# Values of two token tiles at once by a Strassen product in a gated window-attention kernel

## The chip, the cores and the metric

The kernel runs on one core of a Trainium2 chip. The metric is the device time of one execution in microseconds, the median of the runs shown. The core has five engines with an instruction queue each, worked off in order: TensorE (PE, with its weight loads listed as PEld), VectorE (DVE), ScalarE (ACT), GpSimd (POOL) and SyncE (SP, which here only issues DMAs).

## What is computed

The input x has 8 sequences of 1024 tokens with 512 channels, all in float32. With xn the layer norm of x (no scale, no shift), the reference is:

```python
q, k, v = (xn @ W.T + bias for each of Wq, Wk, Wv), cut into 16 heads of 32 channels
scores  = q k^T / sqrt(32), and -1e30 where (i mod 256) < (j mod 256)
s       = (softmax(scores) v, heads joined) @ Wo.T + bo
y       = clip((xn @ sign(weights).T) * scale + bias, -100, 100)
out     = x + s * silu(y)
```

## The kernel before

**Tiles.** A sequence (a batch b) is 8 tiles of 128 tokens. The tokens are permuted so that the mask, which depends on positions modulo 256, becomes a block triangle of tiles. `norm_work` normalises a tile and turns it, so that xnT holds channels on partitions. The products of a batch are: queries and keys (`heads_work`, for each of 4 groups of 4 heads and each half of the tokens), values (`values_work`, for each token tile), the gate y (`gate_work`, for each tile) and the output (`output_work`, for each tile). Apart from the gate each is written by `product` (L339): four chunks of 128 channels, and in each chunk four matmuls of 32 stationary columns side by side, 512 columns wide. They accumulate in one PSUM bank. A product may be cut inside a chunk into two column ranges.

**Steps.** The main loop (L1053) has 8 batches x 4 head groups g x 9 steps n. A step does, in this order on PE:

- `probs_quad`: the *t* matmuls, scores with the row maximum already subtracted, into a tile of four PSUM banks. ACT then takes the exponential of it (L612).
- `attend_quad`: probabilities times values (*av*) of the step before, at some steps `sum_keys`, and filler. This is the first stretch of filler, "gap one".
- at steps 0 and 7 `shift_rows` turns the parts of the row maxima (*mT*, L555), and ACT copies them (L557).
- `maxima_quad`: the *s* matmuls, scores of the next head group, into the same four-bank tile. DVE takes their row maximum (`pm`, L528).
- filler again, "gap two", up to the next step's t matmuls.

POOL adds up the exponentials of a group over the keys (`add_probs`, L643). Step n's additions are issued in step n + 1; there are none for step 0. The probabilities have two buffers beside the two tiles of sums, so an exponential can wait for the additions of two steps before.

**Filler.** Everything else is filler: queries, keys, values, gates, outputs, turns. Its order is written out by hand, one string for each head group (L787 to L804): `V4` is the value product of tile 4, `G2` the gate of tile 2, `q20` the queries of group 2 and half 0, `O4` the output of tile 4 of the batch before, `N0` the norm of a half, `W0` a turn of the output weights, `R` the product that folds the value bias into the output bias; a prime means the next batch, and what stands before a bar may be begun in the group before. `Beside.fill` (L919) takes filler from this list until a wanted cost is reached. An item has a cost in microseconds (0.86 for a chunk, 2.0 for a gate), may be unready, may be split, and may be free (cost 0: loads, splits, finishing operations).

**PSUM.** Eight banks: four for the t and s tile, two for av, and two ("bank", L121) that all filler products and mT share in turn. A bank comes free when its product has been read: values by one ACT copy (L377), queries and keys by one ACT operation with bias (L394), gates by two DVE operations (L426, L427), outputs by two DVE operations (L722, L723), whose result POOL adds to x (L724) before SP stores it, mT and the key sums by an ACT copy.

**Gates.** A gate's xn is split by ACT (L421) and POOL (L422) into two parts, which have two buffers each, and multiplied by the sign weights in two passes.

**Weights.** The turned weights of queries, keys, values, gate and output lie in SBUF all the time.

## Time and profile before

| | us |
|---|---|
| three runs | 2245.12, 2246.44, 2246.84 |
| median | 2246.44 |
| the profiled execution | 2248.59 |
| its span, first to last instruction | 2246.7 |

| engine | busy us | share of the span |
|---|---|---|
| PE | 2196.6 | 98% |
| DVE | 1276.6 | 57% |
| ACT | 876.5 | 39% |
| POOL | 1323.7 | 59% |

Busy time is the time in which an engine executes. PE at 98% is busy, but matmuls side by side overlap, so the sums of single groups are larger than the time they take together. A line of the timeline has the start, the time until the last one ends, engine, line of the code, what is written and read, the form and the count; in brackets is the engine's idle time before it and what ended it. A line of the table by stretches has the stretch, its length, and for PE, PEld, DVE, ACT and POOL the busy time with the count of instructions; then the granted TensorE clock, the DMA share and GB/s. DMA moves 93.55 MB in the span, 42 GB/s.

### The profile page before, as it was taken

Reading aid. Unit: us, or ns where it says so; the run is one execution under the profiler, and the core shown is the slowest. Engines: PE = TensorE matmul, PEld = TensorE weight load, DVE = VectorE, ACT = ScalarE, POOL = GpSimd, SP = SyncE. Lnnn points to the kernel's source line nnn. Section 1 sums busy time; section 2 is a strip of 40 time slices with the busy share of each in tenths; the row PEclk is TensorE's granted clock in tenths of the full one; section 3 lists DMA queues with packets and bytes.
Section 4 is the critical chain, followed back from the end, with each engine's and each line's share of the span. In section 5 each row is a group of like instructions: output and inputs, shape, how many; then the busy total and the mean of one; then the engine's idle time right before and its main releaser. Section 6 shows DMA issues by size and latency. Waiting matters only on the chain. (4 is left out here: it accounts for less than half of the span.)

```text
span 2246.7 us, 56396 instructions
## 1 busy us (share of the span) xinstructions
PE 2196.6 (98%) x25553; PEld 851.8 (38%) x25553; DVE 1276.6 (57%) x1633; ACT 876.5 (39%) x864; POOL 1323.7 (59%) x1198
## 2 busy tenths in 40 slices
PE   8999999999999999999999999999999999999998
PEld 3334333343333433333333333334333343333333
DVE  4556556665556655566555665565655665555664
ACT  2235433434334434344333443334334344333331
POOL 1256566666566666576556665557666566655562
PEclk9999999999999999999999999999999999999999
DMA  4001000120001210012000120002100111000113
GB/s 164 1 16 34 11 6 29 53 76 30 25 25 39 72 33 25 25 62 68 16 25 25 62 67 16 25 26 66 62 16 27 41 62 62 7 20 25 44 53 123
DMA packets 49672, 93.55 MB, mean 42 GB/s; under 512 B 5388, under 2 KB 5656, under 8 KB 49432
## 3 DMA queue, kind: packets, MB, share of 16 engines
q1 hardware_dynamic: 48720, 88.76, 12.0%
q8 instruction: 200, 3.28, 0.6%
q10 hardware_dynamic: 712, 1.19, 0.2%
q14 instruction: 40, 0.33, 0.0%
HBM read 56.37 MB, written 33.55 MB: 40 GB/s over the span
## 5 line engine op out<-in xcount | busy, mean ns | idle before, releaser
L643 POOL TENSOR_TENSOR p<-p,p 128x512 f32<-128x512 f32 x930 | 1096.4, 1212 | 202.7 <-PE av L625 111.2
L528 DVE TENSOR_REDUCE pm<-s 128x4 f32<-128x2048 f32 (+3 forms) x384 | 664.9, 1752 | 608.8 <-PE s L515 605.9
L612 ACT ACTIVATE p<-t 128x2048 f32<-128x2048 f32 x288 | 540.9, 1878 | 856.4 <-PE t L599 797.8
L700 DVE RECIPROCAL aT<-aT 128x128 f32<-128x128 f32 x256 | 230.2, 928 | 222.4 <-ACT aT L661 222.4
L515 PE MATMUL s<-k,q 32*128 32x512 f32 (+3 forms) x3072 | 320.2, 510 | 7.8 <-ACT p L612 6.9
L625 PE MATMUL av<-p,v 128*32 128x512 f32 (+3 forms) x3072 | 308.2, 496 | 1.6 <-DVE aT L704 1.4
L599 PE MATMUL t<-q,k 32*128 32x512 f32 (+3 forms) x3072 | 306.1, 492 | 0.0
L351 PE MATMUL q_ps<-xnT,wqT 128*32 128x512 f32 (+2 forms) x2656 | 254.2, 497 | 5.5 <-ACT xnT L322 4.7
L351 PE MATMUL k_ps<-xnT,wkT 128*32 128x512 f32 (+2 forms) x2784 | 257.2, 487 | 1.1 <-ACT xnT L322 0.7
L351 PE MATMUL v_ps<-wvT,xnT 128*32 128x512 f32 (+3 forms) x2712 | 254.9, 491 | 0.0
L351 PE MATMUL o_ps<-woT,aT 128*32 128x512 f32 (+2 forms) x2584 | 244.6, 501 | 1.7 <-ACT xnT L322 0.7
L724 POOL TENSOR_TENSOR s<-s,xb 128x512 f32<-128x512 f32 x63 | 85.8, 1362 | 245.3 <-DVE s L723 245.3
L428 POOL TENSOR_SCALAR y<-y 128x512 f32<-128x512 f32 x64 | 39.6, 619 | 279.9 <-DVE y L427 265.2
L422 POOL TENSOR_TENSOR x<-xnT,x 128x512 fp32r<-128x512 f32 x58 | 74.0, 1277 | 166.4 <-ACT x L421 164.0
L599 PEld LDWEIGHTS t<-q,k 32*128 32x128 f32 x3072 | 139.1, 185 | 25.8
L351 PEld LDWEIGHTS k_ps<-xnT,wkT 128*32 128x32 f32 x2784 | 82.7, 110 | 170.4 <-issue 142.5
L351 PEld LDWEIGHTS q_ps<-xnT,wqT 128*32 128x32 f32 x2656 | 78.3, 109 | 177.3 <-issue 152.5
L625 PEld LDWEIGHTS av<-p,v 128*32 128x32 f32 x3072 | 70.3, 108 | 195.9 <-issue 163.4
L351 PEld LDWEIGHTS v_ps<-wvT,xnT 128*32 128x32 f32 x2712 | 78.6, 109 | 167.8 <-issue 143.9
L515 PEld LDWEIGHTS s<-k,q 32*128 32x128 f32 x3072 | 116.3, 185 | 59.4 <-ACT p L612 47.5
L449 PE MATMUL y_ps<-fwT,x 128*128 128x512 f32 x464 | 135.5, 418 | 1.7 <-ACT k L394 1.3
L351 PEld LDWEIGHTS o_ps<-woT,aT 128*32 128x32 f32 x2584 | 76.2, 109 | 156.7 <-issue 135.2
(95 smaller groups left out, 1465.2 us busy)
## 6 DMA issues: line engine op xcount, KB each, us to landing
x<-in_L_attn_x_dram SPq DMA_DIRECT2D x64, 256.0 KB, 3.2
g<-t SPq DMA_DIRECT2D x64, 256.0 KB, 2.0
gb<-g SPq DMA_DIRECT2D x64, 256.0 KB, 3.1
xb<-in_L_attn_x_dram SPq DMA_DIRECT2D x64, 256.0 KB, 3.1
out_dram<-s SPq DMA_DIRECT2D x63, 256.0 KB, 2.5
wk_st<-in_L_attn_Wk_dram ACTq DMA_DIRECT2D x2, 512.0 KB, 5.5
wq_st<-in_L_attn_Wq_dram SPq DMA_DIRECT2D x2, 512.0 KB, 4.6
wv_st<-in_L_attn_Wv_dram SPq DMA_DIRECT2D x2, 512.0 KB, 6.4
```

The lines of the kernel that those rows point to most:

```text
L351: nc.tensor.matmul(hold[0][cols, lo:hi], lhsT=lhsT[:, cols], rhs=rhs[:, lo:hi], start=(i == 0 and lo == 0), stop=(i == n - 1), skip_group_ ...
L422: nc.gpsimd.tensor_tensor(part[1], src, part[0].bitcast(F32), ALU.subtract)
L428: nc.gpsimd.tensor_scalar(y[0], y[0], MAX_VAL, -MAX_VAL, ALU.min, ALU.max)
L449: nc.tensor.matmul(hold[0], lhsT=part[i][:, c, :], rhs=wT["fw"][:, c, :], start=(i == 0 and c == 0), stop=(i == 1 and c == NC - 1),)
L515: nc.tensor.matmul(sc[:, h, at : at + w], lhsT=qt[b, g][head_rows(h), i * P : (i + 1) * P], rhs=kt[b, g][head_rows(h), lo:hi], start=not f ...
L528: nc.vector.tensor_reduce(pm[:, 0 if lo == 0 else 1, i, :], sc[:, :, at : at + w], AX.X, ALU.max)
L599: nc.tensor.matmul(sc[:, h, at : at + w], lhsT=kt[b, g][head_rows(h), j * P : (j + 1) * P], rhs=qt[b, g][head_rows(h), q0 : q0 + w], start ...
L612: nc.scalar.activation(pt[:, :, :width], sc[:, :, :width], AF.Exp, scale=SCALE)
L625: nc.tensor.matmul(av[b, g, f][head_rows(h), lo : lo + w], lhsT=vt[b, j][:, g * P + h * DK : g * P + (h + 1) * DK], rhs=pts[b, g, n][:, h, ...
L643: nc.gpsimd.tensor_tensor(t[:, hs, lo : lo + w], t[:, hs, lo : lo + w], p[:, hs, at : at + w], ALU.add)
L700: nc.vector.reciprocal(r, r)
L724: nc.gpsimd.tensor_tensor(s, s, xr, ALU.add)
```

## The change

**Values.** `values_work` is replaced by `values_pair`: the values of two token tiles i and j come from one Strassen product (in Winograd's form) on 2 x 2 blocks. The left blocks X are halves of the channels (2 x 128) of the two tiles, the right blocks A are quarters of the value weights (256 channels by 256 outputs). Seven block products take the place of eight. Each is 2 chunks of 128 channels, 256 columns wide, and so 14 half-wide chunks in place of the 2 x 4 full ones. They go in four phases through four banks, two block products to a bank, the last alone.

**Sums.** POOL makes four differences T of the left blocks for each pair (`prepare`, issued during the pair before). Four sums S of the weight blocks are made once, by DVE, at the start. The block products are combined by seven more sums of 256 columns for each pair: three read only SBUF and run on POOL, four read PSUM and run on DVE; ACT makes four copies of 256 columns in place of two of 512. DVE's first sum reads what POOL has added from the first phase.

**Weights.** Seven weight blocks (128 x 3584 float32) take more room than the value weights did, and now share one tile with the output weights (128 x 2048). Both are kept in DRAM after the start. `Lo` and `Lv` in the strings load one over the other, twice in each batch, on SP.

**Room.** The gate's two parts have one buffer each in place of two, so a gate is split only when the gate before it has been multiplied. The head outputs of the later half have five buffers in place of six.

**Order.** The strings are new: pairs replace single tiles, O4 to O7 stand at the start of group 1 and O0 to O3 at the start of group 2, and the output weights are turned earlier, in group 1 of batch 0. `Beside.fill` may stop ahead of an opening product after a slow bank, and at the end of gap one a slow half-chunk that is next and ready is finished there.

```diff
-    heads = pool("heads", 6)
+    heads = pool("heads", 5)
...
+    part_sums = pool("part_sums", 1)
+    sums_p = pool("sums", 1)
+    wvo = pool("wvo", 1)
...
+    kept_w = pool("kept_w", 1, space=bass.MemoryType.DRAM)
...
+    def sum_blocks():
+        for out, a, b, op in (
+            ("S1", "A21", "A22", ALU.add),
+            ("S3", "A11", "A21", ALU.subtract),
+            ("S2", "S1", "A11", ALU.subtract),
+            ("S4", "A12", "S2", ALU.subtract),
+        ):
+            nc.vector.tensor_tensor(wb[out], wb[a], wb[b], op)
...
+    def keep_weight(name):
+        weight_d[name] = kept_w.tile(list(wb["tile"].shape), F32, tag=name, name=f"{name}_d")
+        nc.sync.dma_start(weight_d[name], wb["tile"])
+        wb["name"] = name
+
+    def load_weight(name):
+        shared_tile(name)
+        nc.sync.dma_start(wb["tile"], weight_d[name])
+        wb["name"] = name
...
-    def values_work(b, it):
...
+            phases = (
+                (("X11", "A11"), ("T2", "S2")),
+                (("T3", "S3"), ("T1", "S1")),
+                (("T4", "A22"), ("X22", "S4")),
+                (("X21", "A12"),),
+            )
...
+                for q in range(NH):
+                    cols = head_rows(q)
+                    nc.tensor.matmul(
+                        hold[k][cols, part * 256 : part * 256 + 256],
+                        lhsT=self.t[lhs][:, c, cols], rhs=wb[rhs][:, c, :],
+                        start=(part == 0 and c == 0), stop=(c == 1), skip_group_check=True,
+                    )
...
+            for out, a, b in (
+                ("T1", "X12", "X11"), ("T2", "X22", "T1"), ("T3", "X22", "X12"), ("T4", "X21", "T2"),
+            ):
+                nc.gpsimd.tensor_tensor(t[out], t[a], t[b], ALU.subtract)
...
+            if k == 0:
+                u[0], u[1] = part_sum(name, 0), part_sum(name, 1)
+                nc.scalar.copy(u[0], ps[:, LO])
+                nc.scalar.copy(u[1], ps[:, HI])
+                later(lambda: plus(u[1], u[1], u[0], nc.gpsimd))
+            elif k == 1:
...
+                plus(u[2], ps[:, LO], u[1])
+                plus(vt[b, j][:, HI], ps[:, HI], u[2])
+                plus(u[3], ps[:, HI], u[1])
+            elif k == 2:
+                y21, y12 = vt[b, i][:, HI], vt[b, j][:, LO]
+                nc.scalar.copy(y21, ps[:, LO])
+                nc.scalar.copy(y12, ps[:, HI])
+                later(lambda: plus(y21, y21, u[2], nc.gpsimd))
+                later(lambda: plus(y12, y12, u[3], nc.gpsimd))
+            else:
+                plus(vt[b, i][:, LO], ps[:, LO], u[0])
...
-                part[i] = parts.tile([P, NC, P], F32R, tag=f"x{i}", name=f"x{i}_{b}_{it}", bufs=2)
+                part[i] = parts.tile([P, NC, P], F32R, tag=f"x{i}", name=f"x{i}_{b}_{it}")
...
     STEADY = (
-        "V4 G2 V5 q20 | V7 G3 V6 k20 q21 G4 k21",
-        "O4 G5 O5 | q30 N0 k30 O6 q31 G6 k31 G7",
-        "N1 O7 O0 | O1 k00' V0' q00' O2 O3 q01'",
-        "k01' V1' | q11' G0' V2' k10' G1' V3' k11' q10'",
+        "V45 G2 | q20 V67 Lo G3 k20 q21 G4 k21",
+        "O4 O5 G5 O6 O7 | q30 N0 k30 q31 G6 k31 N1 G7",
+        "O0 O1 O2 O3 Lv | k00' q00' k01' q01'",
+        "V01' G0' | q11' V23' k10' G1' k11' q10'",
     )
     OPENING = (
-        "V2 G0 V3 V4 G1 V5 V7 V6 G2 k20 q21 k21",
-        "G3 q20 q30 N0 k30 | G4 q31 G5 k31 G6 V0'",
-        "G7 N1 V1' | k00' q00' W0 V2' W1 V3' W2 q01' W3",
-        "k01' G0' R | q11' k10' G1' k11' q10'",
+        "V23 G0 V45 | V67 G1 k20 G2 q21 k21",
+        "G3 W0 q20 W1 G4 | q30 W2 N0 k30 W3 R G5 q31 Lv N1 G6 k31",
+        "G7 V01' | k00' q00' k01' q01'",
+        "G0' V23' | q11' k10' G1' k11' q10'",
     )
     CLOSING = (
-        "V4 V5 | q20 V7 V6 k20 q21 k21",
+        "V45 V67 Lo | q20 k20 q21 k21",
...
+                elif w.opens and shut["banks"] == 2:
+
+                    break
...
-    start += values_work(0, 0)
+    start += [Work(0, sum_blocks), Work(0, lambda: keep_weight("wv")), Work(0, pairs[0].prepare)]
...
-    start += values_work(0, 1)
+    start += pairs[0].halves[0] + pairs[0].halves[1]
...
+        if nxt:
+
+            ahead = next((w for w in now.work if w.cost), None)
+            if ahead and ahead.closes and ahead.slow and ahead.cost < 0.5 and ahead.ready():
+                spent += fill(ahead.cost, kept, 0)
```

## The prediction

> **What bounds the kernel now.** First the busy table. TensorE (PE) is busy 2196.6 of 2246.7 us. The other engines have room, GpSimd (POOL) least, at 59%.

> ```profile
> span 2246.7 us, 56396 instructions
> ...
> PE 2196.6 (98%) x25553; PEld 851.8 (38%) x25553; DVE 1276.6 (57%) x1633; ACT 876.5 (39%) x864; POOL 1323.7 (59%) x1198
> ```

> So the time is the stream of matmuls plus 50 us in which PE idles; by the table of stretches 9.2 of these lie in the first 56 us and 9.4 in the last 47. The same table shows a middle batch: 271.3 us, 269.2 of them busy.

> ```profile
> 1056.90:1328.20 271.30, 269.20 (x3160) 104.13 (x3160) 157.44 (x200) 109.69 (x108) 169.96 (x153) 1.00 0.13 40
> ```

> The timeline prices the stream. Four float32 matmuls run side by side on 32 columns each, and every one is two passes (two records).

> ```profile
> 32.68 3.64 PE L351 MATMUL q_ps<-xnT,wqT 128*32 128x512 f32 x32 [0.68 <-ACT xnT L322]
> ...
> 2234.80 1.48 PE L749 MATMUL o_ps<-woT,aT 128*32 128x256 f32 x24
> ```

> 32 records are eight fours; less the last one's own 0.62 us, (3.64 - 0.62) / 7 = 0.43 us per four at 512 columns. At 256 it is (1.48 - 0.40) / 5 = 0.216: half the columns cost half the time.

> A step has two stretches of filler. Gap one, between the t matmuls and the s matmuls, must cover the exponential (1.88 us) on ScalarE (ACT). Gap two, from s to the next t, must cover the maximum on VectorE (DVE). Both share one four-bank tile. Gap two, just too thin:

> ```profile
> 2171.34 1.92 PE L351 MATMUL y_ps<-fwT,xnT 128*32 128x512 f32 x16
> 2171.49 2.35 DVE L528 TENSOR_REDUCE pm<-s 128x4 f32<-128x512 f32 x2
> ...
> 2173.90 0.39 PE L577 MATMUL t<-shift,neg 3*128 3x512 bf16 x4 [0.64 <-DVE pm L528]
> ```

> 1.7 us of filler, 0.64 of waiting: with less than some 2.1 us the rest is lost. Gap one needs some 2.05 us (steps with 2.04 show no wait). The filler's two PSUM banks are the other limit:

> ```profile
> 423.31 1.88 ACT L612 ACTIVATE p<-t 128x2048 f32<-128x2048 f32 x1 [4.86 <-PE t L599]
> ...
> 424.11 0.40 PE L555 MATMUL mT_ps<-identb,mt 128*128 128x128 bf16 x4
> ...
> 425.08 0.58 ACT L557 COPY shift<-mT_ps 128x512 bf16<-128x512 bf16 x1
> ...
> 425.71 0.53 PE L351 MATMUL q_ps<-xnT,wqT 128*32 128x192 f32 x8 [0.54 <-ACT shift L557]
> ```

> A bank filled in gap one is emptied by ACT only behind the exponential, 2.4 us after the gap begins; whoever needs that bank in the same gap waits.

> **The stream.** Values were 64 products of 4 chunks, two fours each: 256 x 2 x 0.43 = 220.2 us. Now 32 pairs of 14 half-wide chunks: 448 x 2 x 0.216 = 193.5. **-26.6 us** (-22 if a half pass cost 0.221, -28 at exactly half of 0.431). All of it is on PE's path.

> [...]

> **Sums and copies, taken at nothing.** Each pair adds 7 POOL operations of 256 columns. No row has them; 512 columns take 1.286 us and 384 take 1.008, so by the slope 0.73 (bounds 0.62 to 1.008). 7 x 0.73 = 5.1 us a pair, 20.4 a batch, on 170 of 271: 71%. It adds 4 DVE sums reading PSUM at 0.417 (L757) and turns two ACT copies of 0.585 into four of about 0.38. Three sums hold DVE 1.25 us, less than the 1.38 of an output tile's two operations. The cover is that most pairs lie at a head group's start, where step 0 has no additions of probabilities. If it goes, the exponential waits for POOL and PE behind it, one for one. Two new waits lie inside this: the fourth difference of a prepared pair waits on POOL until PE has read the old one, with value sums and the next additions queued behind it; and DVE's first sum waits for POOL's sum of the first phase, with the next maximum behind it. PE reaches both a gap or more after the work they need is issued, so I cost them at nothing (at most 1 us a pair).

> **Single buffers.** A gate's two parts (ACT 0.614, POOL 1.277) can now be made only when the gate before has been multiplied. In the new order gates stand two steps or more apart, about 15 us; nothing, or up to 2 us a gate if POOL is late. The fifth buffer of the later half's head outputs is free once O7 is done, and O4 to O7 now stand in the first steps of group 1, before the sum of keys at step 8 that writes it: nothing.

> **Reloads.** 1.83 MB for values, 1.05 MB for output, per batch, on SP. A 0.5 MB row lands in 4.6 to 6.4 us, so at most 22 and 13 us. The value load is issued when the last O's store ahead of it in the queue is released, and four to five steps of 7.5 us pass before its first use: hidden. Output has more. On SP the gate stores and fetches behind a load wait only until PE has finished the tile's last reader; at the start the loads of the next x stand behind the store of the blocks, which waits for DVE's sums, and they have 100 us. An uncovered load would cost PE its whole landing.

> **New bank waits.** By PE's order in the built program and the bank of each filler product, two places per batch repeat the row at 423 us. At step 0 of group 0 gap one holds attend 0.86, mT 0.33, a pair's last 0.43 of bank 1, then opens bank 2, which is mT's. It wants it 1.6 us into the gap and gets it at 2.4: 0.85 lost. At step 0 of group 3 mT needs the bank of the pair's first phase, closed 0.43 earlier and emptied by two ACT copies behind the exponential: 0.85. Six times each, 10.2. Queued behind each on PE are the s matmuls, and behind those the maximum, so the whole step shifts. Small ones (a gate behind an output tile's DVE operations in group 1) come to 5 x 0.2. **+11.1 us**; 0 if ACT reaches the copies first, 15 if DVE queues too.

> **Waits that go.** In batches 2 to 6 a q product waits 0.675 for the turned x, a gate 0.22, a turn 0.14; the new order puts other work there: 5 x 1.03 = 5.2. This one stands once per batch as well, because output additions and the norm's scale put POOL's sums late:

> ```profile
> 1056.95 1.14 PE L515 MATMUL s<-k,q 32*128 32x512 f32 x8 [0.94 <-ACT p L612]
> ```

> With the O's one per step, POOL's additions end some 3 us ahead of the exponential; I take half of 5 x 0.92. **-7.5** (0 to -10).

> **Opening.** Early filler runs out at the end of batch 0: two gap twos are empty (2 x 2.1) and two gap ones short (0.86, 0.34): 5.4. The first turn of the output weights now waits for a gate's DVE work behind a maximum (1.5); four DVE sums of weight blocks (4 x 0.7) delay one maximum (1.2); POOL's preparation for the third and fourth pair, 1. Its old waits for the turned weight and for a mask bank (1.22, 0.72) go. **+7.2** (4 to 13).

> **End.** The last gates run out sooner: one gap two of 0.86 and an empty one, 1.3 + 2.1 less the 0.64 shown; one of 1.39 (0.75); a mask bank behind a gate (1.2); a short gap one (0.34). **+5.0** (3 to 7).

> Sum: -26.6 + 11.1 - 7.5 + 7.2 + 5.0 = **-10.8 us**. The profiled execution took 2248.6 (span 2246.7), 2.2 more than the median of 2246.4. Taken from the median: **2235.6 us**.

> **Rivals.**

> Nearly all of it arrives. If ACT empties the banks in time, the 11.1 vanish: -21.9, **2224.5**. For it: steps with 2.04 us in gap one have almost no spare, so a small shift of ACT's order would do. Against: the row at 423 us has this very order. Chance 0.17.

> No change. The queues of DVE and ACT give 7 us more back, for instance maxima that wait 0.4 us behind pair sums in ten steps of every batch's groups 0 and 3: **2243**. For it: DVE runs in order and already stands behind output tiles. Against: gap twos there are mostly 2.4 to 2.6 us. Chance 0.14.

> Slower: POOL becomes the bound in groups 0 and 3. At step 3 of group 0 the exponential needs the buffer that POOL's sums of step 1 free. In that queue stand two value sums, a clip that waits for a gate on DVE (done about 7.7 us after the last t), the split of the next gate (1.28), then 4 x 1.286. By these rows they end 0.9 us before the exponential is due. If 256-column operations cost 1.008, a pair brings 2 us more; beyond the 0.9 each microsecond is one of PE, twice a batch. It decides from 1.05 us lost at each of 14 places on (10.8 + 4); at 1.5: -10.8 + 21 = **2256.6**. Against: 29% of POOL stays idle. Chance 0.09.

> That the change doesn't do what it says is excluded for the stream: the program's order has 1792 value matmuls of 256 columns in place of 1356, mostly of 512.

> **Numbers.** A measurement of this kernel can tell about 0.2%, 4.5 us, from no change. Forecast's own case (2230 to 2242): 0.60. Faster: 0.60 + 0.17 = 0.77; same 0.14; slower 0.09. The range goes down to the full gain, 2224, and up to 2246; outside lie the slower case and part of "no change".

> **What would show it.** Value records of 256 columns with fours 0.216 apart; PE's waits with two new lines of about 0.85 us per batch, released by ACT's shift copy and by the copies of the first phase; the q wait of 0.675 gone; three to five waits of about 2 us for DVE pm near the end of batch 0 and in the last gates; a middle batch of 268 to 269.5 us in place of 271.3. The prediction is wrong if ACT's exponential waits for POOL by tens of us beyond today's 58.5, or if the middle batch is not shorter.

## The result

The changed kernel takes **2268.36 us** (median of four runs, 2265.94 to 2272.10) against 2246.64 for the kernel before. The ratio is 1.0099, with a 95% interval of 1.0082 to 1.0117. It was forecast to be 11 us faster and is 22 us slower. The profiled execution of after is the slowest of its four, 2272.1 us; all sums below are made on the two profiled spans, 2270.3 and 2246.7.

The page of after:

```profile
span 2270.3 us, 59421 instructions
...
PE 2176.0 (96%) x26705; PEld 900.2 (40%) x26705; DVE 1354.8 (60%) x1767; ACT 880.3 (39%) x930; POOL 1487.0 (65%) x1422
```

PE works 20.6 us less and the span is 23.6 longer. POOL's extra work is as costed (20.4 us a batch make 163). DVE has grown by 78 us, although its new sums take only 52 us (26.7 + 25.6): remember that. The table by stretches, for batch 0, a middle batch, and four neighbouring windows of 3.41 us in batch 0:

```profile
79.31:371.66 292.35, 269.47 (x3244) 114.80 (x3241) 163.85 (x210) 116.91 (x132) 194.75 (x193) 0.96 0.08 28
...
1186.64:1458.01 271.37, 264.72 (x3309) 110.50 (x3307) 167.42 (x217) 110.05 (x116) 190.45 (x181) 1.00 0.15 51
190.08:193.49 3.41, 1.94 (x20) 0.74 (x16) 1.98 (x1) 3.09 (x6) 3.41 (x4) 1.00 0.00 0
193.49:196.91 3.42, 0.15 (x4) 0.18 (x8) 3.42 (x5) 0.21 (x1) 2.84 (x2) 1.00 0.30 115
196.91:200.32 3.41, 3.41 (x20) 1.09 (x17) 0.48 (x2) 0.00 (x0) 0.00 (x0) 0.50 0.68 274
200.32:203.73 3.41, 3.41 (x64) 1.65 (x60) 0.00 (x0) 1.50 (x1) 0.00 (x0) 1.00 0.00 0
```

Two things are to be seen. The middle batch is as long as before (271.30), with PE busy 4.5 us less: the stream's gain is there and is waited away. And batch 0 ran at a mean clock of 0.96: after a window in which PE worked for 0.15 us, the third line from the end, the clock granted in the next one is 0.50. The first six fours of the bias product start there and take 3.95 us; at full clock (e3 below) they take 2.25. Between 100 and 380 us of after the clock is halved six times, in before not once. So the difference has three parts. "Waits" are PE's gaps over 0.15 us, "half clock" is half of the time at clock 0.50, and the rest is work.

| us | before | after | difference | forecast |
|---|---|---|---|---|
| PE's work | 2198.2 | 2163.5 | -34.7 | -26.6 |
| waits: start, batches 0 and 1 | 20.4 | 41.4 | +21.0 | +15.8 in all |
| waits: batches 2 to 6 | 13.1 | 30.7 | +17.6 | |
| waits: batch 7 and end | 6.9 | 11.7 | +4.8 | |
| half clock: start, batches 0 and 1 | 5.1 | 17.1 | +12.0 | 0 |
| half clock: batch 7 and end | 3.0 | 5.9 | +2.9 | 0 |
| span | 2246.7 | 2270.3 | +23.6 | -10.8 |

The table of waits of after (what PE waited for, total us, times, longest):

```profile
PE t L746 <- DVE pm L697: 21.1, 15, 4.1
PE s L670 <- ACT p L781: 9.4, 15, 1.0
PE k_ps L418 <- ACT xnT L389: 6.1, 9, 0.7
PE y_ps L614 <- DVE v L450: 6.0, 5, 1.2
PE bo_ps L418 <- DVE bvb L941: 4.7, 1, 4.7
PE mT_ps L724 <- ACT v_u L528: 4.4, 6, 0.7
PE v_ps L472 <- ACT shift L726: 3.9, 6, 0.6
```

The last two are the bank waits of the forecast. The first, fourth and fifth are for DVE, and the timeline shows why. Steps are numbered 0 to 35 in a batch. At step 22 of batch 0:

```profile
260.15 9.87 POOL L812 TENSOR_TENSOR p<-p,p 128x512 f32<-128x512 f32 x8
...
261.52 9.05 DVE L600 SCALAR_TENSOR_TENSOR t<-t,y 128x512 f32<-128x512 f32 x1
...
270.50 2.28 DVE L697 TENSOR_REDUCE pm<-s 128x4 f32<-128x2048 f32 x1
...
272.83 0.62 PE L746 MATMUL t<-shift,neg 3*128 3x384 bf16 x8 [4.05 <-DVE pm L697]
```

One DVE operation, the last of a gate, takes 9.05 us. Where no POOL operation runs beside it, it takes 0.68. It reads two operands in SBUF, and here it ends 0.55 us after POOL's eight operations without a pause have ended. The maximum stands behind it, and PE behind the maximum. At step 4 of each of five batches the same happens on a smaller scale, and there the pair's last sum stands behind it, which must empty the bank that the next gate wants:

```profile
943.82 4.98 POOL L812 TENSOR_TENSOR p<-p,p 128x512 f32<-128x512 f32 x4
...
947.06 3.66 DVE L600 SCALAR_TENSOR_TENSOR t<-t,y 128x512 f32<-128x512 f32 x1
...
950.64 0.41 DVE L450 TENSOR_TENSOR v<-v_ps,v_u 128x256 f32<-128x256 f32 x1
...
951.11 1.20 PE L614 MATMUL y_ps<-fwT,x 128*128 128x512 f32 x4 [1.20 <-DVE v L450]
```

The same operation in before, by the table of groups (total, mean ns of one), and in after:

```profile
L435 DVE SCALAR_TENSOR_TENSOR t<-t,y 128x512 f32<-128x512 f32 x64 | 53.6, 839 | 0.0
```

```profile
L600 DVE SCALAR_TENSOR_TENSOR t<-t,y 128x512 f32<-128x512 f32 x64 | 83.1, 1300 | 0.0
```

That it was 839 on average and not 680 in before, where single ones took up to 2.31, could have been read before the change. It doesn't always last to the end of POOL's row, though: 1.45 us beside a row of 15.53 in e6, and the last section.

### The profile page after: what moved, and what is told of

The parts are those of the page before. It is cut to its first block, busy times and chain, and to the rows that moved or that the text cites. A ratio compares the mean times of both kernels' runs of the same rounds, so it can differ in the third digit from the quotient of the medians.

```text
span 2270.3 us, 59421 instructions
## 1 busy us (share of the span) xinstructions
PE 2176.0 (96%) x26705; PEld 900.2 (40%) x26705; DVE 1354.8 (60%) x1767; ACT 880.3 (39%) x930; POOL 1487.0 (65%) x1422
## 5 line engine op out<-in xcount | busy, mean ns | idle before, releaser
L418 PE MATMUL k_ps<-xnT,wkT 128*32 128x512 f32 (+3 forms) x2776 | 256.6, 488 | 6.3 <-ACT xnT L389 6.1
L418 PE MATMUL q_ps<-xnT,wqT 128*32 128x512 f32 (+3 forms) x2808 | 256.4, 482 | 0.9 <-ACT xnT L389 0.7
L418 PE MATMUL o_ps<-wo_shared,aT 128*32 128x512 f32 (+2 forms) x2688 | 243.2, 488 | 0.7 <-DVE aT L875 0.5
L895 POOL TENSOR_TENSOR s<-s,xb 128x512 f32<-128x512 f32 x63 | 85.4, 1356 | 181.5 <-DVE s L894 174.0
L418 PEld LDWEIGHTS o_ps<-wo_shared,aT 128*32 128x32 f32 x2688 | 80.7, 110 | 176.4 <-issue 145.4
L418 PEld LDWEIGHTS q_ps<-xnT,wqT 128*32 128x32 f32 x2808 | 83.6, 110 | 168.7 <-issue 140.7
L746 PE MATMUL t<-shift,neg 3*128 3x512 bf16 (+3 forms) x1536 | 114.9, 330 | 25.6 <-DVE pm L697 21.1
L614 PE MATMUL y_ps<-fwT,x 128*128 128x512 f32 x464 | 127.7, 410 | 8.1 <-DVE v L450 6.0
L472 PE MATMUL v_ps<-wv_shared,v_t 128*32 128x256 f32 x2048 | 127.7, 381 | 5.7 <-ACT shift L726 3.9
```

The costliest lines, as they stand in the source:

```text
L418: nc.tensor.matmul(hold[0][cols, lo:hi], lhsT=lhsT[:, cols], rhs=rhs[:, lo:hi], start=(i == 0 and lo == 0), stop=(i == n - 1), skip_group_ ...
L472: nc.tensor.matmul(hold[k][cols, part * 256 : part * 256 + 256], lhsT=self.t[lhs][:, c, cols], rhs=wb[rhs][:, c, :], start=(part == 0 and ...
L614: nc.tensor.matmul(hold[0], lhsT=part[i][:, c, :], rhs=wT["fw"][:, c, :], start=(i == 0 and c == 0), stop=(i == 1 and c == NC - 1),)
L746: nc.tensor.matmul(sc[:, h, at : at + w], lhsT=neg1[r, :], rhs=shift[b, g, f][r, lo : lo + w], start=(k == 0), stop=False, skip_group_chec ...
L895: nc.gpsimd.tensor_tensor(s, s, xr, ALU.add)
```

## The experiments

The change was taken apart in four kernels, then mended in steps. The kernel before, run beside each set, took 2245.8 to 2246.4.

**e1, no sums on POOL.** Seven POOL operations a pair left out.

```diff
-                nc.gpsimd.tensor_tensor(t[out], t[a], t[b], ALU.subtract)
+                t[out] = t[a]
...
-                later(lambda: plus(u[1], u[1], u[0], nc.gpsimd))
...
-                later(lambda: plus(y21, y21, u[2], nc.gpsimd))
-                later(lambda: plus(y12, y12, u[3], nc.gpsimd))
```

> The changed kernel with the seven POOL operations of each pair left out (the T differences are replaced by the plain blocks, and three of the seven sums are not made, so the values are not the reference's). The order on PE is the same, matmul for matmul. Theory P, POOL's longer queue: a gate's last operation on DVE, two operands in SBUF, lasts 0.68 us alone but 3.66 us at step 4 of every batch and 9.06 us at step 22 of batch 0, each time until POOL's queue pauses; the maximum or the pair's last sum stands behind it on DVE, and PE behind that. Then these go (1.2 us x 5, about 0.7 of the 1.09 us at step 21 x 6, 4.05 us once with 3.4 us of halved clock after it), and with them the s matmuls' waits at steps 13 and 14 (1.37 us x 6) and step 3 of batch 0 (1.88 and 1.7 of clock): about 31 us less than the changed kernel's 2268.4, so 2237, and a middle batch of about 268 us. Rival R, bank hand-overs and the order alone: within 4 us of 2268, middle batch 271.

Measured: 2257.68 us, ratio to before 1.0057 (1.0042 to 1.0072), 10.7 less than after. The direction is P's, the size is a third of it. The operation at step 4 falls from 3.66 to 1.6 us and at step 22 of batch 0 from 9.05 to 0.63, and the waits of 1.2 and 4.05 behind them are gone; so is the wait of 1.88 for POOL's differences at step 3 of batch 0. But the waits at steps 13, 14 and 21 (0.98, 0.38, 1.09) are there as before: they are not the sums' doing, against what I expected. The middle batch is 270.3.

**e2, no last operation of the gates.** It is the victim that goes here; POOL's work stays.

```diff
-            nc.vector.scalar_tensor_tensor(t[0], t[0], 1.0, y[0], ALU.add, ALU.mult)
```

> The changed kernel with the last DVE operation of every gate left out (the tanh is stored in place of the finished gate, so the output is not the reference's); POOL's work is all there. Theory P (DVE's operation on two SBUF operands waits for a pause of POOL, and what stands behind it on DVE makes PE wait): the wait of 4.05 us at step 22 of batch 0 and the two half-clock windows after it go (7.5 us), the 1.2 us at step 4 of five batches go, and part of the 1.09 at step 21: 14 to 18 us less, 2250 to 2254. The waits of the s matmuls at steps 13 and 14 stay. Rival Q (POOL harms only through the buffers of the exponentials): DVE is 0.68 us x 64 shorter, which is off the path, so within 5 us of 2268, and the 4.05 us stay as a wait for the maximum.

Measured: 2250.72 us, 1.0022 (1.0010 to 1.0033), 17.6 less than after, as P has it. The waits of 1.2 at step 4 and of 4.05 are gone; the bank waits and the 0.98 and 1.09 at steps 13 and 21 stay (1.03, 1.15). Two details differ from P: the 0.39 at step 14 went, and no part of the 1.09 did. The middle batch:

```profile
1175.04:1444.84 269.80, 264.60 (x3310) 110.27 (x3307) 157.42 (x209) 110.04 (x116) 188.00 (x181) 1.00 0.16 51
```

**e3, the clock alone.** Idle transposes are put into four waits.

```diff
+        if (b, g, n) in KEEP:
+            keep = bank(f"keep_{g}_{n}")
+            for _ in range(KEEP[b, g, n]):
+                nc.tensor.transpose(keep[:, 0:P], ident, ident)
...
+                for _ in range(36):
+                    nc.tensor.transpose(keep[:, 0:P], ident, ident)
```

> The changed kernel with 94 idle transposes on PE (0.11 us each) placed inside four of its waits in batch 0: 36 ahead of the product that folds the bias, 30 in the second gap of step 22, 14 each in the second gaps of steps 34 and 35. They do nothing else and end before the wait ends, so the waits stay. Theory C (a 3.41 us window in which PE is idle for more than half is followed by windows at half clock): the half-clock windows after these four waits vanish, which cost 1.7, 3.4, 1.7 and 3.4 us: 2258, and the waits are as long as before. Rival: the halved clock hangs on something else, or what it delays is hidden: 2268 or a little more.

Measured: 2259.14 us, 1.0063 (1.0046 to 1.0080), 9.2 less than after (10.2 expected). First batch 0 by stretches, then the place where after waited 4.73 us for the spread of the bias:

```profile
79.83:362.69 282.86, 270.71 (x3339) 123.07 (x3337) 165.07 (x210) 116.84 (x132) 194.20 (x192) 1.00 0.08 29
```

```profile
189.10 4.09 PE L943 MATMUL keep_bo<-ident 128*128 128x128 f32 x36
194.05 2.25 PE L418 MATMUL bo_ps<-wo_shared,bvb 128*32 128x512 f32 x24 [0.85 <-DVE bvb L948]
```

The clock is 1.00 in place of 0.96 and the batch 9.5 us shorter, though PE is held up as long as before (4.09 of idle transposes and 0.85). Work that is good for nothing made the kernel faster. Here the half clock was a cost of its own, beside the waits that it followed.

**e4, full products in the new order.** Each pair is two products as before, with strings, buffers and reloads of after.

```diff
-    class Pair:
...
+            self.halves = [self.one(b, i), self.one(b, j)]
```

> The changed kernel's strings, single gate buffers, five buffers for the head outputs, shared weight tile and reloads, but values by the full products of before (two per pair, one ACT copy each, no POOL or DVE sums). Three differences of weight blocks are made at the start in place of four sums, so that the reloaded tile is as large. Theory P: what the change lost is lost by the sums' load on POOL and DVE, so here a middle batch is that of before or less (270 to 271.5), and only the opening costs something: 2248 to 2258. Rival O (the order, the single buffers or the reloads lose it): a middle batch of 274 us or more, 2270 or above.

Measured: 2281.27 us, 1.0155 (1.0140 to 1.0171). Theory P's 2248 to 2258 is missed by far, and these are nearly rival O's numbers: batches 2 to 6 take 273.7 to 276.9. So the order is no harmless frame, and in it the Strassen product is worth 13 us. But the loss here is mostly one wait of its own, which brings on half a clock in the same batches (up to 3.4 us each); its table of waits has 3.2 as the longest, where after has 1.0:

```profile
PE s L589 <- ACT p L700: 17.2, 9, 3.2
```

The experiment tells that the new order has waits of its own: those of 0.42, 1.09 and 0.68 us at steps 18, 21 and 24 of after's middle batches stand here too, without any Strassen sum. The size of the others in after it doesn't tell, since other lengths of filler put other work beside each other.

**e5, the gates' last operation behind the maximum.**

```diff
-        finish = Work(0, finish, ready=lambda: 0 in t)
+        finish = Work(0, finish, ready=lambda: 0 in t, late=True)
```

> The changed kernel, with each gate's last DVE operation issued at the end of its step, behind that step's maximum, where it stood ahead of it; nothing is left out and the order on PE is the same. Theory P (that operation holds DVE until POOL's queue pauses, and what stands behind it on DVE makes PE wait): behind the maximum it delays nothing that PE needs soon, so the 4.05 us at step 22 of batch 0 with 3.4 us of halved clock, and 1.2 us in each of five batches go, as they did when the operation was left out: 2250 to 2256. Rival: it is as long there and holds up the next gate's or pair's sums, so PE waits at another place: 2262 or more.

Measured: 2263.38 us, 1.0067 (1.0047 to 1.0088), only 5 less, as the rival has it. At step 22 of batch 0 the operation now takes 0.72 and the 4.05 are gone. In the middle batches it starts at the same point as before and takes 3.67: issued at the end of step 3 it stands, like at the start of step 4, between the pair's third and last sum, and DVE reaches neither earlier. So the later issue moved it at step 22 and not at step 4.

**e6, the opening spread out.**

```diff
-            want = max(share, 2.45 if len(S_QUADS[n]) > 1 else 2.35) - spent
+            least = {0: 2.1, 1: 2.15}.get(b, 2.35)
+            want = max(share, least + 0.1 if len(S_QUADS[n]) > 1 else least) - spent
...
-                main = row_work()
+                spread, main = row_work()
+                link(i - 4, spread)
...
+    SECOND = "V45 G2 V67 | q20 Lo G3 k20 q21 G4 k21"
```

> The changed kernel with another distribution of filler in the first two batches: a second gap takes 2.1 us at least in batch 0 and 2.15 in batch 1 (2.35 before), the pair of tiles 6 and 7 may be begun early in batch 1, and the spread of the value bias is issued four items earlier. Theory: the opening's loss is in the two empty gaps (2.41 and 2.76 us, 5.1 of halved clock), two short ones (0.48, 0.67) and the bias product (4.73, 1.7 of clock), and batches 0 and 1 have gaps to spare above 2.1 us that can fill them: 16 us less, 2250 to 2254; the 4.05 us at step 22 stay. Rival: gaps of 2.1 us are too short, or the filler is missing later instead: 2262 or more.

Measured: 2247.70 us, 1.0011 (1.0001 to 1.0020), 20.7 less than after. Batch 0 takes 274.9 in place of 292.4 and batch 1 265.6 in place of 272.3, at a clock of 1.00 in both:

```profile
80.16:355.10 274.94, 263.50 (x3260) 113.14 (x3257) 156.78 (x210) 118.41 (x135) 194.29 (x191) 1.00 0.08 29
```

The steps that had 2.35 us and more of filler had some to give; in batch 0 gaps of 2.1 us leave eight waits of 0.2 to 0.7 for the maximum, in place of the two of 2.41 and 2.76. It is more than expected for two reasons. The operation of 9.05 us at step 22 takes 1.45 here, though POOL's row of additions is longer still:

```profile
252.17 15.53 POOL L812 TENSOR_TENSOR p<-p,p 128x512 f32<-128x512 f32 x13
...
252.56 1.45 DVE L600 SCALAR_TENSOR_TENSOR t<-t,y 128x512 f32<-128x512 f32 x1
```

It got its turn behind the first of the thirteen, and the second took 1.73 us in place of 1.28. So a long row of POOL alone didn't hold it. The other reason is luck: the waits of 1.88 us at steps 3 and 9 stay, but no half clock followed them in this execution, where in after it cost 3.4 us.

**e7, all mended at once**: e5 and e6, the last batch's second gaps at 2.1 us, and `N0` one item earlier.

> The changed kernel mended: the gates' last operation behind the maximum, the first two batches' and the last batch's filler spread thinner (2.1 us at least in the last), the spread of the bias earlier, and the norm of the next batch's first half one item earlier, so that its four small POOL operations do not meet an output's addition at step 13. If the terms add up: 17 us for the first, 16 for the second, 4 to 7 at the end, 0 to 6 for the norm: 2223 to 2231, faster than both kernels. Rival: the waits share one shortage of POOL's time and move on: 2240 or more.

Measured: 2252.66 us, 1.0036 (1.0022 to 1.0051), more than e6 alone. The terms don't add up. The middle batches stay at 271.1 to 273.8, with the waits at steps 13 and 14 still there (1.03, 0.34): the norm's place isn't their cause alone. The profiled execution is the fastest of the five, 2248.57 at a clock of 0.998; the others ran at 0.995 and 0.996. Why more half-clock windows fall into them is not settled.

**e8, each reload twice.**

```diff
+        nc.sync.dma_start(wb["tile"], weight_d[name])
```

> The changed kernel with each reload of the shared weight tile issued twice (5.7 MB a batch in place of 2.9). Theory: the reloads are hidden (a first load lands in 5.8 or 7.9 us, several steps ahead of its use), so within 3 us of 2268. Rival: they delay gate stores, fetches and loads of x on SP's queue and the DMA engines: 5 to 20 us more, with waits on DMA or on the shared weights in the batch.

Measured: 2269.12 us, 1.0097 (1.0082 to 1.0112): 0.8 more than after, no difference. The reloads are hidden.

**e9 and e10, work moved to DVE**, both on top of e6: the three sums of POOL, and the copy of mT.

```diff
-                nc.scalar.copy(y21, ps[:, LO])
-                later(lambda: plus(y21, y21, u[2], nc.gpsimd))
+                plus(y21, ps[:, LO], u[2])
...
-        nc.scalar.copy(t, ps)
+        nc.vector.tensor_copy(t, ps)
```

> The kernel with the spread-out opening (2247.7 us), and the three sums of each pair that POOL makes moved to DVE, which reads them from PSUM (0.41 us each) in place of three of the four ACT copies; the order on PE is the same. Theory P (POOL's unbroken queue holds DVE's operation on two SBUF operands): POOL's run of operations is 2.2 us shorter for each pair, the gate's last operation at step 4 falls from 3.67 us to 2.2 or less, PE's 1.2 us there go (a batch without them took 269.95 in place of 271.4): middle batch 269.9 to 270.3, 2239 to 2243. Rival: the longer row of sums on DVE (1.25 us more a pair) delays the next maximum instead: middle batch 271.4 or more, 2247 or more.

> The kernel with the spread-out opening (2247.7 us), and the copy of the turned row maxima out of its PSUM bank made by DVE in place of ACT, where it stands behind the exponential; the order on PE is the same. Theory B (PE's waits of 0.65 at step 0 and 0.74 at step 27 of each middle batch are for a bank that ACT empties behind the exponential): DVE empties the bank some 1.5 us earlier, the first of the two goes and the second too where the bank waited for is that of the turned maxima: 0.6 to 1.4 us a batch, middle batch 270.0 to 270.8, 2239 to 2244. Rival: DVE stands behind the inverses and the gates' last operation there, and PE waits as long or longer: 2247 or more.

Measured: 2273.36 us, 1.0122 (1.0105 to 1.0138), and 2256.49, 1.0046 (1.0031 to 1.0061). Both rivals hold in their numbers. In e9 the operation at step 4 falls to 1.6 and PE's 1.2 us there go, as expected, but it isn't the maximum that is late: banks that ACT emptied now wait for DVE:

```profile
PE mT_ps L721 <- DVE v_u L450: 13.4, 11, 1.4
...
PE k_ps L418 <- DVE v L450: 11.7, 5, 2.3
```

In e10 the wait of 0.65 at step 0 becomes 1.62, since the reciprocals stand ahead of the copy on DVE. Busy for 61% of the span in both, DVE has no place in these steps.

**e11, both of these and the last batch's thinner gaps.**

> Both of these together, and the last batch's second gaps at 2.1 us at least, which leaves filler for the two thin gaps near its end (1.42 and 2.48 us, 2.9 of halved clock). If the terms add up: 5 to 8 for the sums, 4 to 8 for the copy, 4 to 6 for the end: 2226 to 2234, faster than both kernels. Rival: DVE, with both loads, becomes the queue that PE waits for: 2245 or more.

Measured: 2281.40 us, 1.0158 (1.0141 to 1.0175). The rival again.

**e12, outputs apart**, on top of e6 with the last batch's second gaps at 2.1 us.

```diff
-        "O4 O5 G5 O6 O7 | q30 N0 k30 q31 G6 k31 N1 G7",
-        "O0 O1 O2 O3 Lv | k00' q00' k01' q01'",
+        "O4 O5 G5 O6 q30 O7 | N0 k30 q31 G6 k31 N1 G7",
+        "O0 k00' O1 q00' O2 O3 Lv | k01' q01'",
```

> The kernel with the spread-out opening (2247.7 us), the last batch's second gaps at 2.1 us at least, and the output products no longer one after another: queries or keys stand between O6 and O7, and between O0, O1 and O2. Theory S (in the middle batches the waits of the s matmuls at steps 13 and 14, 1.37 us, and of the t matmuls at step 21, 1.09, come from the output tiles in a row: each brings two operations of 0.69 us on DVE and an addition of 1.3 us on POOL): half or more of them go, 1.2 to 2.4 us a batch, middle batch 269 to 270.2, and with 4 us at the end 2231 to 2238. Rival: these waits come from the additions of probabilities, the norm's scale and the reciprocals, which stay: middle batch 271.4, and 2242 to 2245 by the end alone.

Measured: 2244.83 us, 0.9991 (0.9981 to 1.0000). Half of theory S: the 1.09 us at step 21 are gone, and the middle batch is 270.3; the wait at step 13 stays (1.48, with none at step 14). The 4 us at the end didn't come: the last batch takes 270.7, in e6 270.4.

**e13, the gates' last operation off DVE**, on top of e12.

```diff
+            nc.scalar.activation(t[0], t[0], AF.Identity, bias=ones[:, 0:1], scale=1.0)
...
-            nc.vector.scalar_tensor_tensor(t[0], t[0], 1.0, y[0], ALU.add, ALU.mult)
+            nc.gpsimd.tensor_tensor(t[0], t[0], y[0], ALU.mult)
```

> The kernel before this one in the list (outputs apart, opening and end spread), with the gate's last operation taken off DVE: ACT adds the one (0.6 us) and POOL multiplies (1.29 us); nothing is left out and the order on PE is the same. Theory P: DVE no longer has an operation that waits for POOL's pauses, the waits behind it (1.2 us at step 4 and part of step 21) go, as they did when it was left out (1.5 us a batch): 7 to 10 us less than that kernel. Rival: POOL's longer queue (82 us more) makes the exponentials wait instead: the same or more than that kernel, and s matmuls that wait for the exponential by 2 us a batch more.

Measured: **2240.56 us**, 0.9979 (0.9969 to 0.9988), 4.3 less than e12, where theory P had 7 to 10, and 0.2% faster than the kernel before. The 1.2 us at step 4 are gone. The s matmuls wait 1.03 at step 13 and 0.54 at step 34, in the whole run 9.2 us where e12 has 8.4, though POOL is busy for 69% of the span: the rival's 2 us a batch aren't there. In this profiled execution half clock followed the waits of 1.88 and 1.96 at steps 3 and 9 of batch 0 again, 3.4 us that e12's doesn't have (mean clocks 0.996 and 0.997). The middle batch, in which the two bank waits are still there (0.65, 0.74):

```profile
1162.04:1431.21 269.17, 264.64 (x3309) 110.20 (x3306) 157.34 (x210) 115.48 (x124) 197.87 (x189) 1.00 0.15 51
```

## Why the prediction was wrong

**The stream was right.** From start to next start, without PE's waits, the value matmuls take 240.5 us before and 211.6 after, -28.9 where -26.6 was forecast. PE's other work is some 6 us less too, which was not traced.

**"Sums and copies, taken at nothing" is the step that failed in the middle batches.** POOL's operations were priced well (0.73 to 0.75 us). What was asked was whether they make the exponential late. What was not asked is which operations of other engines last longer while POOL works: the gates' last one on DVE, on two SBUF operands, takes 0.68 us alone and took 9.05 at step 22 of batch 0 and 3.66 to 3.69 at step 4 of five batches, where it ended behind POOL's row of operations. At step 4 POOL's two value sums are the end of that row. Leaving that operation out is worth 17.6 us (e2), with the half clock that it brought on; leaving the sums out 10.7 (e1). A middle batch takes 269.8 us without that operation and 271.4 with it, where 268 to 269.5 were forecast; what is left are the waits that didn't go (below). That the middle batch is no shorter than before was a sign of being wrong that the prediction had named.

Its other sign came as well: ACT's exponential waits for POOL by 26 us more than before.

```profile
ACT p L612 <- POOL p L643: 58.5, 20, 6.5
```

```profile
ACT p L781 <- POOL p L812: 84.8, 32, 6.2
```

But little of this reaches PE: its s matmuls wait for the exponential 12.9 us in after (9.4 and 3.5) and 10.7 in before (6.9 and 3.8). In e1, without the sums and faster, ACT even waits 129.2. The rival "slower" named the right engine, and a victim that explains some 2 us.

**The opening was mis-sized, for two reasons.** The empty gaps (2.41 and 2.76 us), the turn (1.90) and POOL's preparation (1.88) came as named, a little longer than taken (2.1, 2.1, 1.5 and 1). Missed were 4.73 us for the spread of the bias, which in before had stood three items ahead of its product, and the 4.05 at step 22. And every such wait was taken at its own length, while those of 1.88 us and more cost another 1.7 or 3.4 of halved clock in after: 12 us in the opening, 2.9 at the end, 14.8 of the 34 by which the forecast missed. In size this is the larger miss: e6, which changes the order in the first two batches alone, takes back 20.7 of the 22 us, step 22 and its luck included. The end's waits themselves are +4.8, forecast +5.0, in part by luck: those of 1.43, 2.48 and 1.23 us came as named, but 0.96 and 0.51 came unnamed, and a wait of 1.41 for an av product in before is gone.

**"Waits that go" failed too.** The q product's wait for the turned x became one of a k product at step 24 (0.68). The 0.92 us of an s matmul did not halve: there are 0.97 and 0.39 at steps 13 and 14, where the exponential before them waits for POOL's additions, and a new 1.09 at step 21. I argued that outputs one to a step leave POOL time; e12 shows that outputs in a row are what step 21 waits for. What makes POOL late at step 13 is open: e1, e7 and e12 each left it there.

**The new bank waits were right**: 0.65 and 0.74 at the two places named, 8.3 us in six batches, where 10.2 were forecast. The five of 0.2 behind output tiles are not there; five of 0.42 for mT's bank at step 18, behind a gate's DVE operations, came unnamed. The reloads are hidden (e8). The single gate buffers were not tried alone. Two slips in the prediction's sums decide nothing: 190.4 of 271.3 us is 70% for POOL, not 71, and 10.2 and 1.0 make 11.2, not 11.1.

## What to carry to other kernels

Before putting work on an engine with time to spare, list which operations of other engines last longer while it works: here a mean above the shortest duration of one on DVE (839 ns against 680) was the sign. In after's opening the waits of 1.88 to 4.73 us brought 1.7 or 3.4 us of halved clock each, and e6, with many gaps thinned out where after emptied two, took back 20.7 us: price such a wait with the clock behind it. In a kernel whose order is tuned step by step, a new order loses small waits everywhere, and they are found by place, not by engine share.

## What was not expected of the hardware

**DVE beside POOL.** In after, 43 of the 64 last operations of a gate start while a POOL operation runs. Of these, 31 end about 0.55 us after that one operation, and POOL's next, which follows at once, takes 0.3 to 0.5 us longer than usual (such as 1.72 in place of 1.27). Six met the last operation before a pause of POOL. The other six, at step 22 of batch 0 and step 4 of five batches, ended 0.55 us behind POOL's whole row: at step 22 9.05 us over the seven operations of 1.26 that were left of it, six more than the 31 had to let by. DVE's operations that read PSUM kept their length (0.69 on average for 512 columns in both kernels, 0.40 to 0.42 for the value sums of 256). What decides between the two, and by what mechanism, is not shown here.
